# Blocks of adj in the order 2, 3, 0, 1 in the slices of the first product of a graph network kernel

## Chip, cores and metric

The kernel runs on one core of one Trainium2 chip. The metric is the device time of one execution in microseconds. TensorE does matmuls, VectorE, ScalarE and GpSimd (POOL in the profile) do element-wise work, SyncE (SP) issues most of the DMAs; PEld is TensorE's loading of weights.

## What is computed

Four layers, each a graph step with a residual and a normalisation over 64 features. x is 8 x 2048 x 64, adj is 2048 x 2048, all float32:

```python
# layer 0: Chebyshev terms, with weights made per node from an embedding
As = [I, adj, 2 * adj @ adj - I]
x_g = einsum('knm,bmc->bnkc', stack(As), x)
w = einsum('nd,dkio->nkio', embedding, weight); b = embedding @ bias
x = layernorm(x + einsum('bnki,nkio->bno', x_g, w) + b)
# layer 1: two rounds
z = x
for i in range(2):
    z = relu((adj @ z) @ weights[i])
x = layernorm(x + z)
# layer 2
x = layernorm(x + x @ weight_self + (adj @ x) @ weight_neighbor + bias)
# layer 3: Chebyshev terms again, both supports are adj
x = layernorm(x + concat(x, adj x, 2 adj adj x - x, adj x, 2 adj adj x - x) @ weight + bias)
```

Each layer needs two products with adj, or one; in all there are seven. The kernel's first product is adj times x of layer 0, and it is the one that the change is about.

## The kernel before

**Strassen-like products.** A product with adj is done on halves of adj and halves of x, with seven products of quarters in place of eight: adj is cut in quarters A11, A12, A21, A22, and x in quarters by half of the nodes (h) and half of the columns (c). S1 = A21 + A22, S2 = S1 - A11, S3 = A11 - A21, S4 = A12 - S2. Beside them stand T1 = x01 - x00, T2 = x11 - T1, T3 = x11 - x01, T4 = x10 - T2. The products are A11 x00 (pa), A12 x10 (p2), S1 T1 (pc), S2 T2 (pb), A22 T4 (pd), S3 T3 (added onto pb) and S4 x11 (pe). `product` (L189) does this for the later products, in two levels. The sums of blocks of adj that it needs are stored in DRAM (comb, one tensor for each of A11, A12, A22, S1 to S4), and it loads them in the order A11, S1, A12, S2, S4, S3, A22. Within each, the first load is a block of adj itself and the second is comb's block 5.

**The first product makes these sums.** It runs over four slices ns of 512 columns. A slice is four blocks of 1 MB, ch[0] to ch[3], in a ring of four buffers (`slice_chunk`, L141, loads on SP's queue). ch[0] and ch[1] hold the slice's share of A11 and A21, ch[2] and ch[3] that of A12 and A22: the right half of adj. So a buffer is given back when TensorE and VectorE have both read it for the last time.

- Slice 0 is a plain product (`plain_slice`, L607): 64 matmuls of 128x512 with all of x, over the four blocks j = 0 to 3.
- Slices 1 to 3 are fast (`fast_slice`, L631): seven products of two 128x256 halves each (`mul`, L649). The order is pa, p2, pc, pb, pd, S3 onto pb, pe.
- `prepare` (L466) makes the sums of adj of a slice on VectorE in four parts, which `fast_slice` calls with `next(parts)`. `outer` makes S1 to S4 of a slice (two additions of 128x1024 each, in three buffers T), `inner` makes the four second-level sums of one of the seven (four of 128x512, in four buffers C), and `keep` (L481) stores them by a DMA of POOL. Before: part 1 has S1, S2, inner of A11 and S3; part 2 `put(S1)`; part 3 `put(S2)`, S4, inner of A12 and A22; part 4 `put(S3)`, `put(S4)`.
- `sums_of_x` (L573) makes T1 to T4 once, during slice 0. T1 and T3 lie in parts of xy that are written only at the end of the stage, by the transposes of slices 2 and 3; T2 and T4 have their own tiles.
- `done(blk, ps, plus)` (L663) adds two terms into the result hT, half of two of its four tiles: block 0 and 2 into hT of p = 0, 1, block 1 and 3 into p = 2, 3. `back` (L603) then transposes an hT (four matmuls) into xy, from where the second product reads it. Transposes, and matmuls for the bias (`biases`, L550), are held in a list of jobs (`Pump`), and each half of a `mul` gives out one step of it. The transposes of slice 2 are held back until slice 3 has made pc, because they overwrite T1.
- `join_bias` (L580) adds the bias to a quarter of x once its last product has read it, in slice 3. `sum_weights` (L439) and `sum_wn` (L433) prepare the weights of later layers in slices 1 and 2.

**What sets the order.** A planner with a cost model orders the instructions on each engine; program order gives the priorities. An instruction marked by `tc.keep_in_program_order` is pinned to its place among the others so marked. In slices 1 to 3 the sums of adj are pinned, `sum_wn` and `join_bias` too; `sum_weights`, `done` and `plus` (L673) aren't. Each engine and each DMA queue takes its instructions in the order written. SP's queue waits at a load until the buffer is free.

**PSUM in the stage.** Four banks p_n go round over the results of `mul`; slice 0 takes all four, and each fast slice takes six.

Of the kernel before, what the change touches and what calls it, by code (L numbers as in the profile page):

```python
# [16 lines left out]
P = 128  # L17
# [75 lines left out]
def kernel(  # L93
# [53 lines left out]
        return a  # L147

    chunks = {}
    chunks[0, 0] = slice_chunk(0, 0, TG)  # L150
    for t in range(TG):
        nc.scalar.dma_start(xy[:, t, 0, :], x[:, t, :])
    for j in range(1, NG):
        tq = slice(j * TG, (j + 1) * TG)
        nc.sync.dma_start(xy[:, tq, 0, :], x[:, tq, :])
        chunks[0, j] = slice_chunk(0, j)
# [249 lines left out]
    if True:  # L406
# [30 lines left out]
            center(wn.rearrange("p n d o -> p (n d) o"), pin=pin)  # L437

        def sum_weights(w3):  # L439

            for k in range(2):
                half = slice(k * F, (k + 1) * F)
                nc.vector.tensor_tensor(wd[half, W3A, half], w3[half, 1], w3[half, 3], ALU.add)
                nc.vector.tensor_tensor(w3[half, 2], w3[half, 2], w3[half, 4], ALU.add)
                nc.vector.tensor_tensor(wd[half, W3X, half], w3[half, 0], w3[half, 2], ALU.subtract)
                nc.vector.tensor_scalar(wd[half, W3AA, half], w3[half, 2], 2.0, None, ALU.mult)


            for k in range(2):
                half = slice(k * F, (k + 1) * F)  # L450
                center(wd[half, W2N:, half], half)
            for w in (W2S, W3X):
                nc.vector.tensor_tensor(wd[:, w, :], wd[:, w, :], ident, ALU.add)
            for k in range(2):
                half = slice(k * F, (k + 1) * F)
                for n, w in enumerate((W3A, W3X)):
                    nc.vector.tensor_copy(w3o[half, n], wd[half, w, half])
                for n, w in enumerate((W2N, W2S)):
                    nc.vector.tensor_copy(w2o[half, n], wd[half, w, half])
            center(b2.unsqueeze(1))  # L460
            center(b3.unsqueeze(1))

# [1 line left out]
        def prepare(ns, ch, outers):  # L466

            ch = [c.rearrange("p m i n -> p i m n") for c in ch]

            def add(out, a, b, op=ALU.add):  # L470
                inst = nc.vector.tensor_tensor(out, a, b, op)
                if ns:

                    tc.keep_in_program_order(inst)

            def kept(tag, shape, bufs):
                s = sums.tile([P, *shape, GW], F32, tag=tag, name="s" + ("i" if tag == "C" else "o"), bufs=bufs)
                n = "ab"[: len(shape)]
                return s, s.rearrange(f"p {' '.join(n)} (m n) -> p {' '.join(n)} m n", m=TG)

            def keep(q, s0, src):  # L481
                dst = comb[q][s0 : s0 + src.shape[1]].rearrange("s p (n c) -> p s n c", n=TG)
                nc.gpsimd.dma_start(dst[:, :, ns], src)

            def inner(q, q00, q01, q10, q11):
                flat, s = kept("C", (4,), 4)
                add(s[:, 0], q10, q11)
                add(s[:, 1], s[:, 0], q00, ALU.subtract)
                add(s[:, 2], q00, q10, ALU.subtract)
                add(s[:, 3], q01, s[:, 1], ALU.subtract)  # L490
                keep(q, 4, flat)

            def raw(I, J):
                return [ch[2 * J + b][:, 2 * I + a] for a in range(2) for b in range(2)]

            def outer(a, b, op):

                flat, s = kept("T", (2, 2), 3)
                for c in range(2):
                    add(s[:, :, c], a(c), b(c), op)  # L500
                return flat

            def rq(I, J):
                return lambda c: ch[2 * J + c][:, 2 * I : 2 * I + 2]

            def sq(s):
                return lambda c: s[:, :, c].rearrange("p a (m n) -> p a m n", m=TG)

            def put(q, s):
                flat = s.rearrange("p a b c -> p (a b) c")  # L510
                keep(q, 0, flat[:, :2])
                keep(q, 3, flat[:, 3:])
                inner(q, *(flat[:, k].rearrange("p (m n) -> p m n", m=TG) for k in range(4)))

            outers[S1] = s1 = outer(rq(1, 0), rq(1, 1), ALU.add)
            outers[S2] = s2 = outer(sq(s1), rq(0, 0), ALU.subtract)
            inner(A11, *raw(0, 0))
            outers[S3] = s3 = outer(rq(0, 0), rq(1, 0), ALU.subtract)
            yield
            put(S1, s1)  # L520
            yield
            put(S2, s2)
            outers[S4] = s4 = outer(rq(0, 1), sq(s2), ALU.subtract)
            inner(A12, *raw(0, 1))
            inner(A22, *raw(1, 1))
            yield
            put(S3, s3)
            put(S4, s4)
            yield

        with tc.tile_pool(name="p_n", bufs=4, space=PSUM) as p_n, tc.tile_pool(
# [28 lines left out]
            def xq(h, c):  # L560
# [3 lines left out]


            T = [
                xy[:, 2:NT:TG, 1, :].rearrange("p t (h c) -> p t h c", h=2),
                xs.tile([P, NT // 4, 2, 4 * F], F32, tag="T2", name="T2"),
                xy[:, 3:NT:TG, 1, :].rearrange("p t (h c) -> p t h c", h=2),
                xs.tile([P, NT // 4, 2, 4 * F], F32, tag="T4", name="T4"),  # L570
            ]

            def sums_of_x():  # L573
# [33 lines left out]
            def plain_slice(ns, ch):  # L607

                ps = [bank() for p in range(NP)]
                for j in range(NG):  # L610
                    steps = [(p, m) for p in range(NP) for m in range(TG)]
                    if j == 0:

                        steps = [(p, m) for m in range(TG) for p in range(NP)]
                    for k, (p, m) in enumerate(steps):
                        mm = nc.tensor.matmul(  # L616
                            ps[p],
                            xcol(0, TG * j + m, p),
                            ch[j][:, m],
                            start=(j == 0 and m == 0),  # L620
                            stop=(j == NG - 1 and m == TG - 1),
                            skip_group_check=True,
                        )
                        if j == k == 0:
                            tc.keep_in_program_order(mm)
                hT = [new_h() for p in range(NP)]
                for p in range(NP):
                    nc.scalar.copy(hT[p], ps[p])
                return hT

            def fast_slice(ns, ch, held):  # L631
# [44 lines left out]
                    return u  # L676

                next(parts)
                pa = mul(bank(), raw(0, 0), x_of(0, 0))
                p1 = sums.tile([P, GW], F32, tag="p1", name="p1")  # L680
                nc.scalar.copy(p1, pa)
                load_chunks(ns + 1, 0, 1)
                next(parts)
                p2 = mul(bank(), raw(0, 1), x_of(1, 0))
                if ns == TG - 1:
                    join_bias(0, 1)
                    join_bias(0, 0)
                pc = mul(bank(), summed(S1), t_of(1))
                for job in held:
                    pump.add(back(*job))  # L690
                next(parts)
                if ns == 1:
                    sum_weights(w3)
                elif ns == 2:
                    sum_wn()
                pb_ = mul(bank(), summed(S2), t_of(2))
                u2 = plus("u2", pb_, p1)
                done(0, p2, p1)
                pd = mul(bank(), raw(1, 1), t_of(4))
                load_chunks(ns + 1, 2, 3)  # L700
                nc.vector.tensor_tensor(u2, pc, u2, ALU.add)
                next(parts)
                if ns == TG - 1:
                    join_bias(1, 0)
                mul(pb_, summed(S3), t_of(3), start=False)
                u3 = plus("u3", pb_, p1)
                done(3, pc, u3)
                done(2, pd, u3)
                pe = mul(bank(), summed(S4), x_of(1, 1))
                done(1, pe, u2)  # L710
                return [hT[p] for p in range(NP)]

            for ns in range(TG):
                ch = [chunks.pop((ns, j)) for j in range(NG)]
                if ns == 0:
                    for n, _ in enumerate(prepare(ns, ch, {})):
                        if n == 1:
                            sums_of_x()
                    hT = plain_slice(ns, ch)
                    w3 = load_weights()  # L720
                    load_chunks(1, *range(NG))
                    pump.add(biases())
                else:
                    hT = fast_slice(ns, ch, held)
# [222 lines left out]
```

## Time and profile before

| | us |
|---|---|
| median of 3 runs | 1704.3 (1703.21 to 1708.51) |
| the profiled execution | 1703.86 |
| its span, first to last instruction | 1702.1 |
| first product, from 5.69 to the last matmul of slice 3 | to 221.3 |
| of it slice 0 / 1 / 2 / 3 | 55.9 / 59.5 / 50.1 / 50.1 |
| mean granted TensorE clock | 0.997 |
| DMA: mean rate over the span | 230 GB/s |
| DMA: from 0 to 130 us | 334 GB/s |

In the profile a float32 matmul appears as two instructions. "a" stands for any buffer of the ring, "so" for S1 to S4, "si" for the second-level sums, "ps_n" for the banks of the first product. L653 is the matmul of a fast slice, L616 that of the plain slice, L553 the bias matmuls, L336 a transpose, L668 `done`, L146 the load of a block. An engine's idle time is put down to what ended it.

### The profile page before, as it was taken

The page shows a single profiled execution, that of the slowest core. Times are in us where ns is not written, and L with a number is a line of the kernel's source. Part 1 is how long each engine was busy: PE and PEld are TensorE (multiplying, and loading weights), DVE is VectorE, ACT ScalarE, POOL GpSimd, SP SyncE. Part 2 cuts the span into 40 slices and gives each one's busy share as a digit, 9 for nine tenths or more (in the row PEclk, how much of TensorE's full clock was granted, in tenths as well). Part 3 has the DMA queues.
Part 4 walks back from the last instruction along what each step waited for, and adds up shares of the span by engine and source line. Part 5 has one row for each costly group of instructions (what it writes and reads, how often), then busy time and mean ns, then how long its engine had stood idle before and what let it go on. Part 6 is the DMA issues. An engine that isn't in the chain of part 4 may idle for free.

```text
span 1702.1 us, 16167 instructions
## 1 busy us (share of the span) xinstructions
PE 1684.3 (99%) x5952; PEld 853.6 (50%) x5952; DVE 941.9 (55%) x1687; ACT 266.9 (16%) x763; POOL 258.3 (15%) x332
## 2 busy tenths in 40 slices
PE   9999999999999999999999999999999999999997
PEld 4588854444444444444454455554444455554443
DVE  5577885446456546444443365863557444543556
ACT  0000000331333333330011011220001011100001
POOL 1121200443444445450000000000000000000000
PEclk9999999999999999999999999999999999999999
DMA  9898977225222222219877877657878856678883
GB/s 327 334 340 330 333 269 268 93 93 210 87 99 87 99 87 100 87 53 374 305 267 265 309 255 254 224 213 274 295 295 281 304 214 219 224 269 307 312 308 131
DMA packets 82270, 391.23 MB, mean 230 GB/s; under 512 B 8880, under 2 KB 25264, under 8 KB 42640
## 3 DMA queue, kind: packets, MB, share of 16 engines
q1 hardware_dynamic: 69504, 346.78, 57.2%
q0 software_dynamic: 11248, 42.08, 6.4%
q10 hardware_dynamic: 1440, 1.35, 0.2%
q8 instruction: 47, 0.77, 0.2%
q14 instruction: 31, 0.25, 0.0%
HBM read 339.85 MB, written 50.33 MB: 229 GB/s over the span
## 4 chain that ended last, share of the span: by engine, by line
PE 96%; DVE 3%; DMA 1%; ACT 0%; POOL 0%; issue 0%; POOLq 0%
PE mmb L225 25%; PE y L790 20%; PE mmc L225 17%; PE mma L225 16%; PE ps_n L653 8%; PE ps_n L616 3%; PE z L838 2%; PE z L868 2%; PE pt L829 1%; DMA a<-in_slices 1%; PE pt L884 1%; PE pt_n L336 0%; DVE ss L368 0%; DVE sm L352 0%; DVE xy L353 0%; DVE xy L378 0%
## 5 line engine op out<-in xcount | busy, mean ns | idle before, releaser
L225 PE MATMUL mmb<-a,t 128*128 128x512 f32 x1008 | 456.6, 595 | 0.0
L225 PEld LDWEIGHTS mmb<-a,t 128*128 128x128 f32 x1008 | 187.1, 190 | 227.1 <-issue 223.9
L798 DVE SCALAR_TENSOR_TENSOR xy<-y,e_sb,xy 128x128 f32<-128x128 f32 x512 | 179.7, 351 | 123.0 <-PE y L790 107.0
L807 POOL TENSOR_TENSOR s<-s 128x512 f32<-128x512 f32 (+2 forms) x192 | 167.4, 872 | 337.7 <-ACT s L802 327.7
L802 ACT ACTIVATE s<-y,e_sb 128x128 f32<-128x128 f32 x512 | 139.2, 383 | 294.3 <-PE y L790 294.2
L225 PE MATMUL mma<-a,T 128*128 128x512 f32 x384 | 173.5, 594 | 1.7 <-ACT p L240 1.7
L198 DVE TENSOR_TENSOR u<-mmb,p 128x512 f32<-128x512 f32 x84 | 58.0, 690 | 188.3 <-PE mmb L225 188.2
L225 PE MATMUL mmc<-a,t 128*128 128x512 f32 x336 | 152.2, 595 | 0.0
L790 PE MATMUL y<-wn,xT 64*128 64x512 f32 x512 | 135.6, 602 | 0.0
L790 PE MATMUL y<-wn,tT 64*128 64x512 f32 x512 | 131.3, 589 | 0.0
L790 PE MATMUL y<-wn,C 64*128 64x512 f32 x512 | 131.2, 589 | 0.0
L225 PE MATMUL mma<-a,xy 128*128 128x512 f32 x288 | 130.7, 595 | 0.0
L225 PEld LDWEIGHTS mma<-a,T 128*128 128x128 f32 x384 | 71.0, 190 | 87.1 <-issue 84.2
L198 DVE TENSOR_TENSOR C<-mmc,C 128x512 f32<-128x512 f32 x60 | 41.4, 690 | 109.5 <-PE mmc L225 109.5
L225 PEld LDWEIGHTS mmc<-a,t 128*128 128x128 f32 x336 | 61.6, 190 | 71.4 <-issue 71.0
L225 PE MATMUL mmc<-a,T 128*128 128x512 f32 x192 | 86.5, 593 | 0.0
L225 PEld LDWEIGHTS mma<-a,xy 128*128 128x128 f32 x288 | 53.5, 190 | 64.6 <-issue 61.5
L790 PEld LDWEIGHTS y<-wn,xT 64*128 64x128 f32 x512 | 47.1, 186 | 70.2 <-issue 70.2
L790 PEld LDWEIGHTS y<-wn,tT 64*128 64x128 f32 x512 | 49.5, 187 | 60.6 <-issue 60.6
L790 PEld LDWEIGHTS y<-wn,C 64*128 64x128 f32 x512 | 49.6, 187 | 60.3 <-issue 60.1
L240 ACT COPY p<-mma 128x512 f32<-128x512 f32 x42 | 24.6, 586 | 338.3 <-PE mma L225 336.3
L225 PE MATMUL mmc<-a,xy 128*128 128x512 f32 x144 | 65.1, 594 | 0.0
(114 smaller groups left out, 1602.8 us busy)
## 6 DMA issues: line engine op xcount, KB each, us to landing
a<-comb SPq DMA_DIRECT2D x240, 1024.0 KB, 4.8
a<-in_blocks SPq DMA_DIRECT2D x54, 1024.0 KB, 4.9
comb<-si POOLq DMA_DIRECT2D x28, 1024.0 KB, 10.2
a<-in_slices SPq DMA_DIRECT2D x15, 1024.0 KB, 8.1
comb<-so POOLq DMA_DIRECT2D x16, 512.0 KB, 5.6
comb<-so POOLq DMA_DIRECT2D x16, 256.0 KB, 5.6
t1T<-hT SPq DMA_DIRECT2D x16, 256.0 KB, 4.6
xT<-in_xT SPq DMA_DIRECT2D x16, 256.0 KB, 3.1
```

The source lines that it names most:

```text
L198: nc.vector.tensor_tensor(out, a, b, op)
L225: nc.tensor.matmul(ps, xb[:, m, :], a[:, :, m, :], start=(start and m == 0), stop=(m == TG - 1), skip_group_check=True,)
L240: nc.scalar.copy(p1, pa)
L616: mm = nc.tensor.matmul(ps[p], xcol(0, TG * j + m, p), ch[j][:, m], start=(j == 0 and m == 0), stop=(j == NG - 1 and m == TG - 1), skip_gr ...
L653: nc.tensor.matmul(ps[:, ts(p, GW // 2)], b(k, p), a(k // TG, k % TG), start=(start and p == k == 0), stop=(k == NT // 2 - 1), skip_group_ ...
L790: nc.tensor.matmul(y[:, b, :], terms[n][half, ts(k, P)], wn[half, n, h * DH : (h + 1) * DH, :], start=(n == 0), stop=(n == 2),)
L798: nc.vector.scalar_tensor_tensor(acc, y[:, :, ts(d, F)], e, acc, ALU.mult, ALU.add)
L802: nc.scalar.activation(s[:, d], y[:, :, ts(d, F)], AF.Copy, scale=e)
L807: nc.gpsimd.tensor_tensor(s[:, :n], s[:, :n], s[:, n : 2 * n], ALU.add)
L829: nc.tensor.transpose(pt[:, ts(k, P)], xy[:, g * TG + k, slot, ts(p, 2 * F)], ident)
L838: nc.tensor.matmul(z[:, k, :], aT[:, ts(k, P)], wd[:, w, :], start=(n == 0), stop=(n == len(terms) - 1),)
L868: nc.tensor.matmul(z[n][:, k], xT[half, ts(k, P)], w[half], start=True, stop=True)
```

## The change

The blocks are taken in the order `AHEAD` = 2, 3, 0, 1, in the loads of slice 0 and slice 1 and in the plain slice. In a fast slice, the order of the products becomes p2, pd, pa, pc, pb, pe, S3 onto pb. Blocks 2 and 3 of the next slice are loaded after pd, and 0 and 1 after the sum S3. The parts of `prepare` are now five: inner of A12 and A22, S1, S2, S4; `put(S1)`; `put(S2)` and inner of A11; S3; `put(S3)` and `put(S4)`. The results are put together in another way: q3 = pd + p1, p1 becomes p1 + pc, and blocks 3 and 2 are pb + p1 and pb + q3, which are written after the last product. The transposes of slice 2 are given out after pd, whose T4 now lies where T1 lay. The weight sums of slice 1 are pinned.

```diff
@@ -147,10 +147,12 @@
         return a
 
     chunks = {}
-    chunks[0, 0] = slice_chunk(0, 0, TG)
-    for t in range(TG):
+
+    AHEAD = (2, 3, 0, 1)
+    chunks[0, AHEAD[0]] = slice_chunk(0, AHEAD[0], TG)
+    for t in range(AHEAD[0] * TG, AHEAD[0] * TG + TG):
         nc.scalar.dma_start(xy[:, t, 0, :], x[:, t, :])
-    for j in range(1, NG):
+    for j in AHEAD[1:]:
         tq = slice(j * TG, (j + 1) * TG)
         nc.sync.dma_start(xy[:, tq, 0, :], x[:, tq, :])
         chunks[0, j] = slice_chunk(0, j)
@@ -437,28 +439,29 @@
             center(wn.rearrange("p n d o -> p (n d) o"), pin=pin)
 
         def sum_weights(w3):
+            pin = tc.keep_in_program_order
 
             for k in range(2):
                 half = slice(k * F, (k + 1) * F)
-                nc.vector.tensor_tensor(wd[half, W3A, half], w3[half, 1], w3[half, 3], ALU.add)
-                nc.vector.tensor_tensor(w3[half, 2], w3[half, 2], w3[half, 4], ALU.add)
-                nc.vector.tensor_tensor(wd[half, W3X, half], w3[half, 0], w3[half, 2], ALU.subtract)
-                nc.vector.tensor_scalar(wd[half, W3AA, half], w3[half, 2], 2.0, None, ALU.mult)
+                pin(nc.vector.tensor_tensor(wd[half, W3A, half], w3[half, 1], w3[half, 3], ALU.add))
+                pin(nc.vector.tensor_tensor(w3[half, 2], w3[half, 2], w3[half, 4], ALU.add))
+                pin(nc.vector.tensor_tensor(wd[half, W3X, half], w3[half, 0], w3[half, 2], ALU.subtract))
+                pin(nc.vector.tensor_scalar(wd[half, W3AA, half], w3[half, 2], 2.0, None, ALU.mult))
 
 
             for k in range(2):
                 half = slice(k * F, (k + 1) * F)
-                center(wd[half, W2N:, half], half)
+                center(wd[half, W2N:, half], half, pin=pin)
             for w in (W2S, W3X):
-                nc.vector.tensor_tensor(wd[:, w, :], wd[:, w, :], ident, ALU.add)
+                pin(nc.vector.tensor_tensor(wd[:, w, :], wd[:, w, :], ident, ALU.add))
             for k in range(2):
                 half = slice(k * F, (k + 1) * F)
                 for n, w in enumerate((W3A, W3X)):
-                    nc.vector.tensor_copy(w3o[half, n], wd[half, w, half])
+                    pin(nc.vector.tensor_copy(w3o[half, n], wd[half, w, half]))
                 for n, w in enumerate((W2N, W2S)):
-                    nc.vector.tensor_copy(w2o[half, n], wd[half, w, half])
-            center(b2.unsqueeze(1))
-            center(b3.unsqueeze(1))
+                    pin(nc.vector.tensor_copy(w2o[half, n], wd[half, w, half]))
+            center(b2.unsqueeze(1), pin=pin)
+            center(b3.unsqueeze(1), pin=pin)
 
 
 
@@ -512,17 +515,19 @@
                 keep(q, 3, flat[:, 3:])
                 inner(q, *(flat[:, k].rearrange("p (m n) -> p m n", m=TG) for k in range(4)))
 
+
+            inner(A12, *raw(0, 1))
+            inner(A22, *raw(1, 1))
             outers[S1] = s1 = outer(rq(1, 0), rq(1, 1), ALU.add)
             outers[S2] = s2 = outer(sq(s1), rq(0, 0), ALU.subtract)
-            inner(A11, *raw(0, 0))
-            outers[S3] = s3 = outer(rq(0, 0), rq(1, 0), ALU.subtract)
+            outers[S4] = s4 = outer(rq(0, 1), sq(s2), ALU.subtract)
             yield
             put(S1, s1)
             yield
             put(S2, s2)
-            outers[S4] = s4 = outer(rq(0, 1), sq(s2), ALU.subtract)
-            inner(A12, *raw(0, 1))
-            inner(A22, *raw(1, 1))
+            inner(A11, *raw(0, 0))
+            yield
+            outers[S3] = s3 = outer(rq(0, 0), rq(1, 0), ALU.subtract)
             yield
             put(S3, s3)
             put(S4, s4)
@@ -564,10 +569,10 @@
 
 
             T = [
-                xy[:, 2:NT:TG, 1, :].rearrange("p t (h c) -> p t h c", h=2),
+                xs.tile([P, NT // 4, 2, 4 * F], F32, tag="T1", name="T1"),
                 xs.tile([P, NT // 4, 2, 4 * F], F32, tag="T2", name="T2"),
                 xy[:, 3:NT:TG, 1, :].rearrange("p t (h c) -> p t h c", h=2),
-                xs.tile([P, NT // 4, 2, 4 * F], F32, tag="T4", name="T4"),
+                xy[:, 2:NT:TG, 1, :].rearrange("p t (h c) -> p t h c", h=2),
             ]
 
             def sums_of_x():
@@ -607,9 +612,9 @@
             def plain_slice(ns, ch):
 
                 ps = [bank() for p in range(NP)]
-                for j in range(NG):
+                for n, j in enumerate(AHEAD):
                     steps = [(p, m) for p in range(NP) for m in range(TG)]
-                    if j == 0:
+                    if n == 0:
 
                         steps = [(p, m) for m in range(TG) for p in range(NP)]
                     for k, (p, m) in enumerate(steps):
@@ -617,11 +622,11 @@
                             ps[p],
                             xcol(0, TG * j + m, p),
                             ch[j][:, m],
-                            start=(j == 0 and m == 0),
-                            stop=(j == NG - 1 and m == TG - 1),
+                            start=(n == 0 and m == 0),
+                            stop=(n == NG - 1 and m == TG - 1),
                             skip_group_check=True,
                         )
-                        if j == k == 0:
+                        if n == k == 0:
                             tc.keep_in_program_order(mm)
                 hT = [new_h() for p in range(NP)]
                 for p in range(NP):
@@ -676,38 +681,41 @@
                     return u
 
                 next(parts)
+                p2 = mul(bank(), raw(0, 1), x_of(1, 0))
+                pd = mul(bank(), raw(1, 1), t_of(4))
+                load_chunks(ns + 1, 2, 3)
+                for job in held:
+                    pump.add(back(*job))
+                next(parts)
                 pa = mul(bank(), raw(0, 0), x_of(0, 0))
                 p1 = sums.tile([P, GW], F32, tag="p1", name="p1")
                 nc.scalar.copy(p1, pa)
-                load_chunks(ns + 1, 0, 1)
-                next(parts)
-                p2 = mul(bank(), raw(0, 1), x_of(1, 0))
+                q3 = plus("u3", pd, p1)
+                done(0, p2, p1)
                 if ns == TG - 1:
                     join_bias(0, 1)
-                    join_bias(0, 0)
+                next(parts)
                 pc = mul(bank(), summed(S1), t_of(1))
-                for job in held:
-                    pump.add(back(*job))
                 next(parts)
+                load_chunks(ns + 1, 0, 1)
                 if ns == 1:
                     sum_weights(w3)
                 elif ns == 2:
                     sum_wn()
+                else:
+                    join_bias(0, 0)
                 pb_ = mul(bank(), summed(S2), t_of(2))
                 u2 = plus("u2", pb_, p1)
-                done(0, p2, p1)
-                pd = mul(bank(), raw(1, 1), t_of(4))
-                load_chunks(ns + 1, 2, 3)
                 nc.vector.tensor_tensor(u2, pc, u2, ALU.add)
+                nc.vector.tensor_tensor(p1, pc, p1, ALU.add)
                 next(parts)
+                pe = mul(bank(), summed(S4), x_of(1, 1))
+                done(1, pe, u2)
                 if ns == TG - 1:
                     join_bias(1, 0)
                 mul(pb_, summed(S3), t_of(3), start=False)
-                u3 = plus("u3", pb_, p1)
-                done(3, pc, u3)
-                done(2, pd, u3)
-                pe = mul(bank(), summed(S4), x_of(1, 1))
-                done(1, pe, u2)
+                done(3, pb_, p1)
+                done(2, pb_, q3)
                 return [hT[p] for p in range(NP)]
 
             for ns in range(TG):
@@ -718,7 +726,7 @@
                             sums_of_x()
                     hT = plain_slice(ns, ch)
                     w3 = load_weights()
-                    load_chunks(1, *range(NG))
+                    load_chunks(1, *AHEAD)
                     pump.add(biases())
                 else:
                     hT = fast_slice(ns, ch, held)
```

## The prediction

> **What bounds the kernel now.** I read five views in this order: busy time by engine, who TensorE waited for, the chain that ended last around the longest of these waits, a table of short stretches around it, and VectorE's order in time at the end of the first product.
>
> Busy time of each engine, from the profile page:
> ```profile
> PE 1684.3 (99%) x5952; PEld 853.6 (50%) x5952; DVE 941.9 (55%) x1687; ACT 266.9 (16%) x763; POOL 258.3 (15%) x332
> ```
> TensorE is busy for 1684.3 of 1702.1 us. Only 17.8 us are idle, so no reordering can gain more than that, plus any slow clock. The idle time, by what ended it:
> ```profile
> PE ps_n L653 <- DMA a<-in_slices: 2.6, 1, 2.6
> PE rise L539 <- POOL ident masks.py:199: 2.1, 1, 2.1
> PE mma L225 <- ACT p L240: 1.7, 1, 1.7
> PE pt L829 <- DVE xy L378: 1.1, 2, 0.7
> PE pt L884 <- DVE C L198: 1.1, 1, 1.1
> ```
> These are 8.6 us; the other 9.2 us are the tail after the last transpose (1692.26 + 0.66 to 1702.1). Just one wait lies in the stage that is changed: 2.6 us for a block of adj. The chain of waits around it:
> ```profile
> 61.77 13.62 DMA a<-in_slices
> 75.38 0.04 issue
> 75.43 3.40 PE ps_n L653 x8
> 78.82 1.26 PE pb L553 x8
> 80.08 3.65 PE ps_n L653 x16
> 83.74 1.03 PE pb L553 x8
> 84.77 3.65 PE ps_n L653 x16
> ```
> The last block of slice 1 is asked for at 61.77, when the plain slice's last matmul (61.57) gives its ring buffer back, and lands 13.62 us later. Half of p2 used the block before it, until 72.82. The 8 matmul instructions after the wait take 3.40 us. Sixteen otherwise take 3.46. They ran at half rate:
> ```profile
> 60.00:70.00 10.00, 10.00 (x47) 7.59 (x45) 0.73 (x1) 0.68 (x2) 0.64 (x1) 1.00 1.05 381
> 70.00:75.00 5.00, 2.82 (x16) 2.20 (x15) 1.15 (x5) 0.49 (x1) 0.00 (x0) 1.00 0.71 248
> 75.00:80.00 5.00, 4.57 (x16) 3.40 (x16) 4.40 (x7) 0.00 (x0) 1.28 (x2) 0.66 0.22 82
> ```
> Columns: stretch and length, then PE, PEld, DVE, ACT, POOL, the granted clock, the DMA share, GB/s. The clock is 0.66 after the wait. The DMA engines are full until 70 (1.05) and run dry by 75: the block was about the last thing moved.
>
> **Size of the stall with its echo.** From the starts of L653 on TensorE: slice 1 61.57, slice 2 121.09, slice 3 171.19, end 221.30. Slices 2 and 3 take 50.1 us, slice 1 59.52. Of the 9.42 more, four groups of bias matmuls explain 4 x 1.22 = 4.9 (a group is 1.03, and the 16 matmuls after it take 3.65, not 3.46). The rest, 4.5 us, is the stall: 2.6 of waiting, 1.9 of slow clock.
>
> **What the Trainium skill says.** "TensorE: Matmul & The Clock Gate", Part 1, says that an idle window of about 3.4 us halves TensorE's clock, that about 3.4 us of work restores it, and that the window runs free. This trace has a drop after 2.6 us already, while the 1.68 us wait at 766.8 is followed by eight matmuls in 3.70 us, not half rate. So I price the echo as measured, 1.9, and expect none after a gap of 1.7 us or less. "DMA: Bandwidth & Descriptors", section "Issuing engines are not separate DMA queues", says that transfers of all issuing engines share the same 16 DMA engines; this trace's full share at 45 to 70 us, with stores of sums and loads of adj mixed, agrees. So I judge lateness of a block by total bytes, not by its queue.
>
> **The change part by part.**
>
> *Work.* Before and after, a fast slice makes seven products of 3.46 x 2 = 6.9 us. Bias groups and transposes remain four each per slice. VectorE gets one more sum of 128x512 (0.69 us) per slice; it is 55% busy. TensorE's work is unchanged: 0.
>
> *Loads and plain slice.* Blocks and x still come one by one at the same sizes, only as 2, 3, 0, 1. The plain slice needs its four at 5.7, 19.6, 33.6 and 47.6 (14 us each); before, the last had landed by 29.67, when VectorE first read it. 0.
>
> *Slice 1.* The buffer that is freed last, at 61.57, now belongs to block 1, not block 3. TensorE first makes p2 and pd, which read blocks 2 and 3 alone, with the four bias groups: 61.57 + 4 x (3.46 + 1.22) = 80.3. Then pa uses block 0 for 1.73: block 1 is due at 82.0. Before, block 3 was due at 72.82. If it lands at 75.4 again, there are 6.6 us to spare. But VectorE, idle from 60.7 to 72.8 before, may now make the sums of A12 and A22 in that time; POOL stores them, 2 MB more. At the 0.4 MB/us that was moved then this is 5 us. Even if block 1 came behind all of it: 75.4 + 5 = 80.4, still before 82.0. Gain: 4.5, all of it.
>
> *T4 and T1.* pd needs T4 at 70.8 instead of 100.4. T1 to T4 are 4 x 2.29 us of VectorE in slice 0 and were made by 37; held transposes wait for pd where they waited for pc. 0.
>
> *VectorE inside the slices.* S3's sum waits for pc (its buffer is S1's), then the pinned weight sums, then u2 must read pb before S3's product overwrites that bank. After pc ends: S3 2.3, the sums of wn in slice 2 (1.2 + 0.7 + 3.3 + 3.3 = 8.5), u2 0.7, together 11.5; S3's product starts 13.8 after pc. 2.3 us to spare; in slice 1 the weight sums are about 6.5 and there is more. 0. PSUM: pb takes p2's bank, which done(0) frees about 2.5 us after pa; pb starts 7.8 after it. 0.
>
> *SP's queue.* Loads for blocks 2, 3 of the next slice move behind pd, those for 0, 1 behind S3's sum. They are due a full slice later (about 35 us) and half a slice later. With the longest landing of 15.2 us: 0.
>
> *Hand-over to the second product.* Here the change costs. Before, the last product is pe and only done(1) follows it; hT for p = 0 and 1 had been ready from 216:
> ```profile
> 215.66 1.08 DVE L668 TENSOR_TENSOR hT<-ps_n,u 128x256 f32<-128x256 f32 x3
> 221.50 0.76 DVE L668 TENSOR_TENSOR hT<-ps_n,u 128x256 f32<-128x256 f32 x2 [4.76 <-PE ps_n L653]
> 222.17 2.28 DVE L584 TENSOR_TENSOR xy<-xy,pb 128x2048 f32<-128x2048 f32 x1
> ```
> So TensorE went straight on with transposes. After, S3's product is last and all four hT wait for it: done(3) twice, done(2) twice, 0.41 each at a pitch of 0.35. From TensorE's end: first hT at 0.45, the fourth at 1.5. Lower bound of the idle time: the planner takes hT in the order they come, 0.5. Upper: it begins with p = 0, the third to come (1.2), and then waits for a copy of a transpose buffer with nothing between (0.4): 1.6. The matmuls of the next product that read finished tiles may fill in, as two did before (222.36). I take 1.0. There is no echo below 1.7.
>
> **Sum.** Profiled execution 1703.86 (span 1702.1 and 1.8 around it). 1703.86 - 4.5 + 1.0 = 1700.4. The median of the runs shown, 1704.3, is 0.4 above the profiled one, so this is a change of about -0.2%. A measurement of this kernel tells 0.3% (5.1 us) from no change; my forecast is inside.
>
> **Rivals.**
> 1. *More than the stall goes.* The hand-over is filled completely (-4.5: 1699.4) and another of the small waits moves, say the 1.7 us at L225, since the planner orders everything anew: 1697.7. For: two fills were seen at 222 and 226. Against: nothing in the diff aims there.
> 2. *The stall stays or only moves.* Block 1 lands at about 84.6, or S3's sum in slice 0, now last, lets block 0 go late as well. The same 2.6 + 1.9 with the hand-over 1.0: 1704.9; with half the wait and no echo 1702. Against: the byte count above.
> 3. *Slower.* A11's sums of slice 3, stored by 179.5 + 10 before, are now behind done(0) on VectorE. In slice 3, starting at 166.7: pa ends 21.6 later, 188.3; done(0), a bias join and S2's sums are 6.5; A11's own 2.4: 197.2. Store 10.2 and load 4.9: 212.3, while the second matmul group of the next product wants it at about 221.5. There are 9 us to spare. From a store that lands after 217 TensorE waits, and SP's later loads queue behind; from 219.5 on the 3.5 us gained, less the echo, are gone. If VectorE lags by 17 us, the stall is 8 + 1.9 and the time 1710.3. For: VectorE waited 3.8 and 3.1 us for stores in slice 0, and its order is now pinned in more places. Against: it was idle for 6.3 and 4.8 us in slice 3.
>
> **How the numbers follow.** Forecast 0.57 (its own range 1699.3 to 1701.5), rival 1 0.18, rival 2 0.12, rival 3 0.13. The predicted time is the forecast's, 1700.4. From 1697.7 (rival 1) to 1704.9 (rival 2's end) leaves out rival 3 and little else. Faster by over 0.3% is below 1699.2: rival 1, and 0.12 of the forecast where the hand-over is nearly free and the median of runs falls low: 0.30. Slower: rival 3, 0.13. The same: 0.57.
>
> **What would show it.** Right: no wait of L653 for in_slices, slice 1 of about 55 us, the clock at 1.0 between 75 and 80, and a gap of 0.5 to 1.6 us on TensorE before the first transposes at about 217. Wrong: a wait of L653 at about 82 (block 1), a wait in slices 2 or 3 on VectorE's u2, a gap over 2 us at the hand-over with a clock below 1.0 after it, or a wait of mmb for comb.

## The result and the profile after

| | before | changed |
|---|---|---|
| median | 1705.38 us (5 runs, the three shown above and two more, 1703.21 to 1708.51) | 1700.05 us (5 runs, 1699.63 to 1700.68) |
| profiled execution | 1703.86 | 1700.05 |
| its span | 1702.1 | 1697.5 |

The ratio is 0.9968, with a 95% interval of 0.9955 to 0.9981: the change saves 0.32%. The spread shrinks too, from 5.3 us to 1.1.

Busy time by engine of the changed kernel, from its page:
```profile
PE 1681.7 (99%) x5952; PEld 852.3 (50%) x5952; DVE 944.8 (56%) x1690; ACT 266.2 (16%) x763; POOL 258.1 (15%) x332
```
TensorE runs as many instructions as before, and is 2.6 us less busy. Of this, 1.9 is the slow clock of slice 1 that is gone. The rest is about the 0.8 us by which the plain slice was shorter (55.04 us, before 55.88); what shortened it no run here shows, and it varies by as much from one execution to the next (e10 and e11 below). TensorE's waits (total, times, longest):
```profile
PE rise L544 <- POOL ident masks.py:199: 2.1, 1, 2.1
PE mma L227 <- ACT p L242: 1.7, 1, 1.7
PE pt L837 <- DVE xy L380: 1.1, 2, 0.7
PE pt L892 <- DVE C L200: 1.1, 1, 1.1
PE pt_n L338 <- DVE hT L673: 0.7, 1, 0.7
```
The 2.6 us for a block of adj are no longer there. One new line stands in the list, 0.7 us for hT. The other four are the old ones, with the same values. The chain of waits at the start of slice 1 has no DMA in it now:
```profile
61.10 3.45 PE ps_n L658 x16
64.55 1.03 PE pb L558 x8
65.58 3.65 PE ps_n L658 x16
69.23 1.03 PE pb L558 x8
70.26 3.65 PE ps_n L658 x16
73.91 1.03 PE pb L558 x8
74.94 3.65 PE ps_n L658 x16
78.59 1.03 PE pb L558 x8
79.62 3.65 PE ps_n L658 x16
```
The table of stretches (columns as before: PE, PEld, DVE, ACT, POOL, clock, DMA share, GB/s) shows full speed and a DMA that stays full for 5 us longer:
```profile
70.00:75.00 5.00, 5.00 (x28) 4.17 (x28) 0.00 (x0) 0.00 (x0) 0.00 (x0) 1.00 1.02 373
75.00:80.00 5.00, 5.00 (x26) 4.21 (x27) 0.32 (x1) 0.00 (x0) 0.00 (x0) 1.00 0.50 180
```
The clock between 75 and 80 is 1.00, where it was 0.66. VectorE's order in time at the hand-over:
```profile
216.35 0.76 DVE L673 TENSOR_TENSOR hT<-ps_n,p 128x256 f32<-128x256 f32 x2 [3.88 <-PE ps_n L658]
217.03 0.75 DVE L673 TENSOR_TENSOR hT<-ps_n,u 128x256 f32<-128x256 f32 x2
```
done(3) comes first, then done(2). TensorE makes the transposes whose data is there, and waits for the second pair with the others:
```profile
216.15 0.60 PE L338 MATMUL pt_n<-ident,hT 128*128 128x128 f32 x4
217.50 0.77 PE L338 MATMUL pt_n<-ident,hT 128*128 128x128 f32 x4 [0.74 <-DVE hT L673]
```

Where the 4.6 us of span went, by the starts of instructions on TensorE in both traces:

| stretch | before | changed | difference |
|---|---|---|---|
| to the end of the plain slice | 61.57 | 60.94 | -0.63 |
| slice 1 | 59.52 | 55.01 | -4.51 |
| slices 2 and 3 | 100.21 | 100.20 | 0 |
| hand-over, to the first matmul with xT | 5.53 | 6.36 | +0.83 |
| the rest | 1475.27 | 1474.99 | -0.28 |

The saving lies in slice 1. The first row is no effect of the change: that time varies by more than this between executions of one kernel (e10 and e11).

### The profile page after: what moved, and what is told of

Its sections match the earlier page's. It is cut to its first block, busy times and chain, and to the rows that moved or that the text cites. A ratio compares the mean times of both kernels' runs of the same rounds, so it can differ in the third digit from the quotient of the medians.

```text
span 1697.5 us, 16162 instructions
## 1 busy us (share of the span) xinstructions
PE 1681.7 (99%) x5952; PEld 852.3 (50%) x5952; DVE 944.8 (56%) x1690; ACT 266.2 (16%) x763; POOL 258.1 (15%) x332
## 4 chain that ended last, share of the span: by engine, by line
PE 96%; DVE 3%; ACT 0%; POOL 0%; issue 0%; POOLq 0%
PE mmb L227 25%; PE y L798 20%; PE mmc L227 17%; PE mma L227 16%; PE ps_n L658 9%; PE ps_n L621 3%; PE z L846 2%; PE z L876 2%; PE pt L837 1%; PE pt L892 1%; PE pt_n L338 0%; DVE ss L370 0%; DVE sm L354 0%; DVE xy L355 0%; DVE xy L380 0%; PE pb L558 0%
## 5 line engine op out<-in xcount | busy, mean ns | idle before, releaser
L227 PEld LDWEIGHTS mmc<-a,t 128*128 128x128 f32 x336 | 61.5, 190 | 71.4 <-issue 71.0
```

What stands on the lines that cost most here:

```text
L227: nc.tensor.matmul(ps, xb[:, m, :], a[:, :, m, :], start=(start and m == 0), stop=(m == TG - 1), skip_group_check=True,)
```

## Experiments

Theory A says that the gain is cover: two products stand before the first use of the block loaded last. Theory B gives it to the pinned weight sums, theory C to the order of the loads alone. The experiments ran in three rounds, each beside the kernel before, whose median was 1706.79 us (26 runs) for e1, e2, e3 and e6, 1704.83 (38 runs) for e4, e5, e7 and e8, and 1705.78 (39 runs) for e9 to e11. A ratio is to the kernel before of the same round, and not simply that of the two medians. Each trace is of one execution.

**e2: pd back behind pa.**

```diff
                 p2 = mul(bank(), raw(0, 1), x_of(1, 0))
+                next(parts)
+                pa = mul(bank(), raw(0, 0), x_of(0, 0))
                 pd = mul(bank(), raw(1, 1), t_of(4))
...
-                next(parts)
-                pa = mul(bank(), raw(0, 0), x_of(0, 0))
```

> The changed kernel with pd put back behind pa: p2, pa, pd. Loads, sums of adj and weight sums stay as changed. Theory A (cover): what removed the stall is that two products stand before the first use of the block that is loaded last. With one product, block 1 of slice 1 is due at 61 + 2 x 4.68 + 1.7 = 72.1 us, and it landed at 79.7 in the changed kernel: a wait of 7 to 8 us for in_slices in slice 1, a clock drop after it, and a time of about 1708 to 1710. Theory B (VectorE): the gain came from the pinned weight sums, which held VectorE from 60.7 to 72.8 before; it expects no wait here and 1700. Theory C (order of the loads alone): also no wait, 1700.

Measured: median 1710.29 us (20 runs, 1707.07 to 1715.3), ratio to the kernel before 1.0025 (1.0017 to 1.0033). TensorE's first wait, and the chain around it, in e2:
```profile
PE ps_n L658 <- DMA a<-in_slices: 5.5, 1, 5.5
```
```profile
61.45 16.50 DMA a<-in_slices
77.95 0.04 issue
77.99 3.72 PE ps_n L658 x8
```
The block landed at 77.95, earlier than in the changed kernel, and TensorE waited because it wanted it two bias groups and a product earlier. Slice 1 took 62.50 us, 7.5 more than without a stall: 5.5 of wait and 2.0 of slow clock. This execution, of 1707.07 us, was the fastest of the 20, so the stall was probably longer in most of them. B and C fall: the pins and the order of loads are in this kernel, and it is slower than before. The reordered loads without pd as cover are a loss.

**e4: the pins alone, on the kernel before** (`sum_weights` as in the change, nothing else).

> The kernel before with one part of the change alone: the weight sums of slice 1 are pinned to their place. Theory A: TensorE waits for a block of adj and not for VectorE, so the wait for in_slices in slice 1 stays at 2.6 us or more and the time is that of the kernel before, within 0.2%. Theory B, that the weight sums were what made slice 1 late (VectorE stood still from 60.7 to 72.8 on their data), expects the wait to go and a time near 1700.

Measured: 1704.33 us (12 runs), ratio 0.9998 (0.9989 to 1.0008). TensorE's wait and the chain in e4:
```profile
PE ps_n L654 <- DMA a<-in_slices: 3.5, 1, 3.5
```
```profile
61.31 14.53 DMA a<-in_slices
75.84 0.04 issue
75.88 3.78 PE ps_n L654 x8
79.67 1.90 PE pb L554 x8
81.56 5.46 PE ps_n L654 x16
87.02 1.03 PE pb L554 x8
```
The stall stays. B falls a second time. The three pieces after the wait take 3.78, 1.90 and 5.46 us instead of 1.73, 1.03 and 3.65: this time the slow clock cost 4.7 us, not 1.9. The execution, of 1707.38 us, was the slowest of the twelve.

**e5: the changed kernel without the pins.**

> The changed kernel without the pins: the weight sums of slice 1 are free to move, as before. Theory A: no wait of TensorE for in_slices, time 1699.5 to 1700.7 as with the pins. If the pins matter (the planner puts a weight sum ahead of the sums of adj, and VectorE stands still there until its data has landed at about 75 us), the sums of S1 and S2 for pc and pb slip by up to 1 us, still with 2 us or more to spare, so the time stays too; Theory B expects the time of the kernel before.

Measured: 1699.8 us (6 runs, 1699.66 to 1700.47), ratio 0.9971 (0.9960 to 0.9982), no wait for in_slices. The pins are worth nothing here.

**e6: the late load left out, on the kernel before.**

```diff
-                    load_chunks(1, *range(NG))
+                    load_chunks(1, 0, 1, 2)
+                    chunks[1, 3] = chunks[1, 2]
```

> The kernel before, in which slice 1 takes block 2's data in place of block 3's: the load of block 3 of slice 1, which TensorE waits for, is left out, and so the output lacks that block's share in slice 1. All products, sums and stores are done as before. Theory A: the wait for in_slices (2.6 us) and the half-rate clock after it (1.9 us) go, there is no hand-over cost, and the time is 4.5 us under the kernel before as profiled: about 1699.3. The rival, that the stall hides another wait just behind it (the sums of adj or the weights, which VectorE made late before), expects a wait of TensorE for VectorE in slice 1 and a time between 1700.5 and 1704.

Measured: 1698.98 us (4 runs, 1698.71 to 1699.77), ratio 0.9956 (0.9942 to 0.9970). No wait of TensorE on VectorE took the place of the one removed. Nor did the DMA engines have less to do then: the next load in the queue, of the same size, was issued at 61.35 instead and landed at 79.4, and nothing waited for it. So it is the wait for the block that costs, and this is what the stall costs when nothing is paid for its removal: by the ratio, some 7.5 us in the median of this round.

**e3 and e7: what makes block 1 land late.** In the changed kernel block 1 landed 18.5 us after its issue; the block that was last before the change took 13.6. e3 moves the sums of A12 and A22 behind those of S1 in all slices:

```diff
-            inner(A12, *raw(0, 1))
-            inner(A22, *raw(1, 1))
...
             put(S1, s1)
+            inner(A12, *raw(0, 1))
+            inner(A22, *raw(1, 1))
```

> The changed kernel with the sums of A12 and A22 moved from the first part of a slice to behind those of S1. Theory A with its count of bytes: in the changed kernel block 1 of slice 1 landed 18.5 us after its issue instead of 13.6, because 2 MB of stores of these sums went out in the same time. Without them it lands at about 75 to 76 us (first read of it by VectorE), the slack before TensorE's use at 81.3 grows from 1.6 to about 6 us, and the time stays: 1699.5 to 1700.6. The rival, that the landing is late for another cause (the order of the loads on SP's queue), expects the landing to stay at 79 to 80. If VectorE's order matters more than I think, the time rises by over 1 us.

Measured: 1700.55 us (5 runs), as expected, but block 1 landed at 80.7, again 18.5 us after its issue. The landing went against my expectation. The edit wasn't clean: slice 0's sums had moved as well. Their stores had gone out from 20 us on, and now the first second-level sums were stored at 38.9; two stores of 1 MB were issued at 61.5 and 62.8, so the bytes met the load anyway. e7 moves the sums in slices 1 to 3 only (`if not ns:` before the first pair, `if ns:` before the second).

> The changed kernel with the sums of A12 and A22 moved behind those of S1 in slices 1 to 3 alone; slice 0 stays as changed. In e3 they moved in slice 0 too, so their stores left the time from 20 to 40 us, where the DMA engines had room, and met the load of block 1 all the same. Here nothing but the 2 MB of slice 1 leaves the time before block 1's landing. Count of bytes: VectorE's first read of block 1 of slice 1 comes at 75 to 76 us instead of 79.7; the time stays between 1699.5 and 1700.7, since TensorE did not wait for the block before. The rival, that the landing depends on what slice 0 left over and not on these stores, expects 79 to 81 us again.

Measured: 1700.3 us (7 runs). VectorE's first read of block 1, in the changed kernel and then in e7:
```profile
79.68 1.23 DVE L474 TENSOR_TENSOR so<-a 128x1024 f32<-128x1024 f32 x1 [14.59 <-DMA a<-in_slices]
```
```profile
75.09 1.22 DVE L474 TENSOR_TENSOR so<-a 128x1024 f32<-128x1024 f32 x1 [14.41 <-DMA t1T<-hT]
```
It comes 4.6 us earlier. The profile puts the wait in e7 down to a store of hT that was issued just after the load; the load itself landed at 75.0, 12.6 us after its issue. So the 2 MB of stores in slice 1 cost the block 4 to 6 us (it took 18.5 in the changed kernel's first profile and 16.3 in e10), and the count of bytes had 5. The time doesn't move, since TensorE's use at 81.4 in the changed kernel was behind the landing already.

**e1: done(2) before done(3).**

> The changed kernel with one edit: the last two results of a fast slice are written in the other order, done(2) and then done(3). My theory of the hand-over: TensorE waits there (0.7 us for hT in the changed kernel's profile) because the transposes wanted first, those of p = 0 and 1, hang on done(2), which is third and fourth in VectorE's queue. With done(2) first, its wait for hT falls from 0.7 to at most 0.2 us and the time from 1700.05 to about 1699.4. The rival, that the hand-over costs what it costs because any product that ends in four additions delays all of the next product, expects the wait for hT to move to the other pair and the time to stay at 1700.0 or over.

Measured: 1700.31 us (5 runs, 1699.39 to 1700.6): nothing gained. The wait for hT went, but the planner then put twelve transposes in a row instead of eight:
```profile
PE pt_n L338 <- ACT xy L339: 0.3, 1, 0.3
```
From the start of slice 1 to the first mmb (the first matmul of the second product into its tile mmb) it is 163.5 us, in the changed kernel 163.6. That the wait for hT went followed my theory; the time of 1699.4 did not. The rival's move of that wait to the other pair didn't come either.

**e8: the product of S4 last again**, with S3's in a bank of its own:

```diff
-                nc.vector.tensor_tensor(p1, pc, p1, ALU.add)
+                nc.vector.tensor_tensor(q3, pb_, q3, ALU.add)
...
-                pe = mul(bank(), summed(S4), x_of(1, 1))
-                done(1, pe, u2)
...
-                mul(pb_, summed(S3), t_of(3), start=False)
-                done(3, pb_, p1)
-                done(2, pb_, q3)
+                pf = mul(bank(), summed(S3), t_of(3))
+                done(3, pf, u2)
+                done(2, pf, q3)
+                pe = mul(bank(), summed(S4), x_of(1, 1))
+                done(1, pe, u2)
```

> The changed kernel with the last two products of a fast slice exchanged and S3's product in a bank of its own: pb, S3, then pe. Block 3 is S3's result + u2, block 2 is S3's + q3 with pb added to q3, block 1 is pe + u2; VectorE makes as many additions as changed. As in the kernel before, only done(1) follows the last product. My theory of the hand-over: its cost in the changed kernel is 0.8 us (from the end of the last product to the first mmb 8.2 us, before 7.4), and it goes here: no wait of TensorE for hT, 7.4 us, a time of about 1699.2. The rival, that S3's sum, which waits for pc, is now too late for S3's product, expects a wait of TensorE on VectorE between pb and S3 of 0.5 to 2 us in each of the three slices and 1701 to 1705.

Measured: 1703.15 us (21 runs, 1702.09 to 1705.52), slower than the changed kernel by 3 us, though the hand-over is free: from the last product's end (217.6) to the first mmb (225.0) it is 7.4 us. TensorE's longest wait in e8, then VectorE's line behind it:
```profile
PE mmb L227 <- DVE u L200: 2.5, 1, 2.5
```
```profile
228.40 0.69 DVE L200 TENSOR_TENSOR t<-xy,t 128x512 f32<-128x512 f32 x1 [3.69 <-DMA t1T<-hT]
```
Neither theory had this. The second product's t takes a buffer that an hT still holds, until it is stored (as t1T). SP issued that store only after two loads of tT, which read t1T back and were waiting for the stores of the other two hT:
```profile
214.03 1.34 SPq L600 DMA_DIRECT2D t1T<-hT  x2
222.79 1.10 SPq L780 DMA_DIRECT2D tT<-t1T  x2
223.98 1.21 SPq L600 DMA_DIRECT2D t1T<-hT  x2
```

**e9: in e8, POOL issues those two stores.**

```diff
-                nc.sync.dma_start(
+                (nc.gpsimd if ns == TG - 1 and p > 1 else nc.sync).dma_start(
```

> e8 with one edit: in slice 3 the stores of hT for p = 2 and 3 are issued by POOL, not SP. In e8 the hand-over itself cost nothing, but 17 us after it VectorE waited 3.7 us for such a store to give a buffer t back, and TensorE then 2.5 us for VectorE: SP issued these two stores only at 224, behind two loads of tT that waited from 214 to 222.8 for the stores of p = 0 and 1. POOL has nothing else to do there, so the stores go out at about 218.5 and land by 225. My theory: the wait of VectorE falls to 1 us or less, TensorE's 2.5 us go, and the time is that of e8 less 2.5 to 3, about 1699.5 in its median, 0.5 us or more under the changed kernel. The rival, that the landing is slow because the DMA engines are full of loads of adj then (8.9 us for the slowest store in e8), expects a wait of VectorE of 2 us or more to stay and a time of 1701 to 1702.

**e10: the changed kernel beside it.**

> The changed kernel again, beside e9 on one chip, for the difference between the two and for a second profile of it. Theory A: no wait for in_slices, 1699.6 to 1700.7, and slice 1 of 55.0 us; the plain slice ends within 1 us of 61, early or late with TensorE's clock at its start.

Measured: e9 1699.36 us (15 runs, 1698.68 to 1700.02), ratio 0.9964 (0.9955 to 0.9973); e10 1700.05 us (17 runs, 1699.19 to 1701.17), ratio 0.9968 (0.9959 to 0.9976). In e9 VectorE's wait is 1.0 us, TensorE's is gone, and the median is 0.7 us under the changed kernel's. The ranges overlap, so this rests on the medians and on the trace, in which the hand-over's 0.8 us have gone: 7.4 us from the last product's end to the first mmb, in e10 8.2. In e10 slice 1 takes 55.02 us, from 62.03 to 117.05; its plain slice ended 1.1 us later than in the first profile.

**e11: the kernel before again.**

> The kernel before again, for a second profile: its times spread over 10 us where the changed kernel's spread over 1. Theory A: the spread is the length of the wait for block 3 and of the slow clock after it. This execution's slice 1 is then 55.0 us plus a stall, and its time is 1699.3 plus that stall, within 1 us, whatever its length; all else has the same length as in the first profile within 1 us.

Measured: 1704.97 us (12 runs, 1703.17 to 1709.85). The profiled execution took 1704.89, with
```profile
PE ps_n L653 <- DMA a<-in_slices: 4.7, 1, 4.7
```
Slice 1 is 61.66 us, 6.65 over 55.0. 1699.3, the first profile less its stall, and 6.65 are 1705.95, which is 1.06 us too much: just outside the 1 us that I had allowed. The plain slice ended 1.08 us earlier than in the first profile, also just outside; with that it is 1704.87. So one kernel lost 4.5 us to this stall in one execution and 6.65 in another.

That the stall makes the whole spread, of up to 10 us, two profiles can't show. The clock of the runs points the same way: of the 103 runs of the kernel before in the three rounds, the 10 with a mean clock of 0.998 have a mean span of 1699.5 us, the 9 with 0.994 one of 1707.0, and all 22 runs of the changed kernel have 0.998. 0.004 of 1702 us is 6.8 us, so slow clock may be the larger part of the spread. This is an estimate, and at most: the clock is given to 0.001, which is 1.7 us, and a low clock costs nothing while TensorE waits: in e2 it was 0.50 between 75 and 80 us, and TensorE waited until 77.99. The shortest run of the kernel before took 1699.6 us; there the stall can have cost little.

## Why the prediction held, point by point

- *What bounds the kernel, and the stall.* Right. Slice 1 fell by 4.51 us against 4.5 predicted, with the clock at 1.00, and e6 and e2 show that the block's lateness is the cause. One reading was off without harm: 61.57 is the start of slice 1's first matmul, and the plain slice's last one starts at 61.14.
- *Block 1 in time.* Right, and the bound was needed: predicted by 80.4 at the latest, landed at 79.7, 1.7 us before TensorE's use at 81.4. In e10 the margin was 3.9. e2 shows what one product less of cover does.
- *VectorE.* Right for TensorE: it waited for no sum of adj and no u2 in slices 1 to 3. In slice 2, u2's read of pb ended at 153.8, 5.4 us before S3's product at 159.2; I had allowed 2.3, because I put all of the wn sums ahead of u2, and the planner put u2 between them.
- *Hand-over.* Right: 0.83 us measured against 1.0, with an idle time of 0.74 inside the 0.5 to 1.6 given. That the planner's order would be one of the two that I priced was wrong: it transposed what it could of p = 0 and 1 before the wait.
- *Rivals.* Of rival 1, the hand-over wasn't filled, and the wait of 1.7 us for p stayed. Rival 2's late block 1 didn't come, by the margin above. For rival 3, the load of A11's sums was issued at 202.2, I had it at 207.4, and there is no wait for comb.
- *The sum.* 1700.4 predicted, 1700.05 measured. This time doesn't depend on how long the stall is, since I took the stall off the very execution in which I had read it; the gain does. That the two lie within 0.4 us is in part luck: the plain slice (-0.63), the rest (-0.28) and the time around the span (2.55 us, before 1.76) were no terms of the sum, and nearly cancel. The term that was off is the stall in the median. I took the 4.5 us of one execution and set the change at -0.2%, inside 0.3%; it is -0.32%, just past that mark. The traces of before and of e11 have waits of 2.6 and 4.7 us and slow clocks of 1.9 and 2.0 after them; e4, whose stall has the same cause, has 3.5 and 4.7. So the stall in three executions is 4.5, 6.65 and 8.2 us (the last from the slowest run of e4). 4.5 is the lowest of these, the median of before lies 1.5 us above its profiled execution, and e6 puts the stall in the median at some 7.5 us.

Not tried: a fifth buffer of the ring.

## What to carry to other kernels

When a buffer is given back only at the end of a stage, the transfer into it is late by its own length; put work that needs only the other buffers ahead of its first use, and count that cover against all bytes that go out in the same time. A wait read from one profiled execution is one sample: if the times of a kernel spread far more than those of its neighbours, the wait may be much longer in the median, here some 7.5 us with its slow clock where the profile had 4.5. And what a product costs at the end of a stage shows at the hand-over, where results, stores and buffer reuse all hang on it (0.8 us here, 2.5 of another kind in e8).

## What the runs showed that I had not expected

- The slow clock after a wait isn't fixed, and doesn't grow with the wait: 1.9, 2.0, 2.0 and 4.7 us after waits of 2.6, 4.7, 5.5 and 3.5. After 2.49 us, in e8, eight matmuls took 3.70 us: no slow clock at all. Why e4's lasted so long no run shows.
- The plain slice ended between 60.5 (e11) and 62.3 us (e8) with the same 128 matmul instructions.
- Two stores behind two waiting loads on SP's queue (e8) cost 2.5 us of TensorE 17 us later; moved to POOL's (e9), nothing.
